# One chunk of offsets ahead of the first sampling, binarised weights beside the second, and the first convolution in half steps

## The chip, the core and the metric

The kernel runs on one NeuronCore of a Trainium2 chip. The metric is the device time of that core in microseconds (us), as the median of a kernel's executions that were not in a slow state. The kernel before takes 8729 us. A difference of less than 2% counts as "same". A stage length or a single wait below is read from one profiled execution of a kernel.

Engines: PE is TensorE (matmuls; PEld its weight loads), DVE is VectorE, ACT is ScalarE, POOL is GpSimd, SP is SyncE, which here only issues DMAs. "Granted clock" (PEclk) is the share of full speed that TensorE's throttle allowed. All data are fp32.

## The reference, cut to what matters

Four residual layers follow one another on `x` of shape (4, 256, 64, 64), each behind a group norm. Only the first and the weights of the third are touched by the change:

```python
# layer 0, per image (256 channels, 64x64 pixels)
y      = leaky_relu(bn(conv1x1(gn(x))))               # "first convolution"
xp     = y @ inproj_w.T + inproj_b                    # becomes the table that is sampled
t      = leaky_relu(bn(depthwise3x3(y)))
offset = t @ off_w.T + off_b;  mask = softmax(t @ mask_w.T + mask_b)   # 4 groups x 9 points
dout   = (grid_sample(pad(xp), ref + offset) * mask).sum(points)       # bilinear, by gathers
x2     = bn(y + dout @ outproj_w.T + outproj_b)
...                                                   # squeeze-excite, feedforward, residual
# layer 1: linear attention with a 5x5 depthwise convolution
# layer 2: a 3x3 convolution with binarised weights
scale  = mean(|w|, axis=(in, ky, kx)); b = scale * sign(w); c = clip(w, -1, 1)
bin_w  = (b - c) + c
# layer 3: non-local attention (softmax over pooled positions)
```

## The kernel before: the parts that matter

**The order of the whole.** A front (setup, binarising, first convolution and offsets of image 0) is followed by four sampling stages, one per image, and a tail without sampling. A sampling stage has 293 rounds; each round issues four gathers (indirect DMAs from POOL), 1172 in a stage. Other work goes beside it: `beside` takes, after each round, as many pieces from the generators of other work as their shares allow. Inside `ordered()` each engine executes in exactly this order.

```python
def beside(steps, number, *works):
    spent, open_ = [0] * len(works), set(range(len(works)))
    def advance(share):
        for j in sorted(open_):
            work, total, lo, hi = works[j]
            while j in open_ and lo <= share and spent[j] < total * (share - lo) / (hi - lo) or share >= hi:
                cost = next(work, None)          # one piece of work is emitted here
                if cost is None: open_.discard(j)
                if not cost: break               # 0: it has to wait for something
                spent[j] += cost
    for i, _ in enumerate(steps, 1):
        advance(i / number)
    ...

def prepare(images):
    pads, used = [], []
    n = len(images)
    return [((y for i in images for y in self.convolve(i, w, sp, bp, pads, used)), n * CONVOLVE, 0, 1 - 0.12 / n),
            (self.shifts(images, w["mw"], bp, pads, used), n * OFFSETS, 0.2 / n, 1)]

self.setup()
self.binarise()
beside(range(64), 64, *prepare([0]))                               # the front
with ordered():
    beside(self.sample(0, ssum[0]), rounds, *prepare([1, 2, 3]))   # sampling stage 0
    beside(self.sample(1, ssum[1]), rounds, *behind(0))            # stage 1, and so on
```

Note the condition of the `while`: it catches up. When the offsets had to wait (a piece of cost 0) and fall behind their share, all that is missing comes in one round.

**First convolution and offsets.** An image has eight blocks of 512 pixels and four chunks of 1024. Per block and half, the convolution makes two matmuls (four records in the trace) into a PSUM bank, a piece of the memory that matmuls write and ACT and DVE read. ACT and DVE take the result (leaky), the rows go into padded chunks, and a projection writes the table with sixteen DMAs.

```python
def convolved(b, x, yb, m):
    ps = self.ps()                                   # the pool of PSUM banks that all share
    for k in range(KT):
        nc.tensor.matmul(ps, cw[:, k, m*P:(m+1)*P], x[:, k], start=k == 0, stop=k == KT - 1)
    self.leaky(bp, yb[:, m], ps, sh[:, m:m+1], low[:, m:m+1])      # ACT, then DVE: at once
    self.spread({c: p[:, m] for c, p in own.items()}, rw(yb[:, m]), b, 1)
# projected(): two blocks of matmuls, DVE adds the bias, then per block
    for r in range(2):
        for s in range(2):
            for j in range(4):
                nc.sync.dma_start(tab[:, yi, 1:W+1, s, :]..., xo[...])   # 64 KB each

def offsets(...):                                    # per chunk
    for k in range(KT):
        yield from self.depthwise(...)               # DVE: 9 taps of 128x1024, three a piece
        nc.scalar.activation(t[:, k], acc, ...)      # ACT
        nc.vector.tensor_tensor(t[:, k], acc, t[:, k], ALU.max)
    for h in range(2):                               # PE: matmuls ps <- mw, t; DVE adds the bias
        ...
    yield from self.coordinates(...)                 # softmax, indices, weights; then one store
```

**The gathers.** `g` has seven buffers, so POOL may be seven rounds ahead of the matmuls that read them:

```python
g = self.gp.tile([P, G, 256], F32, name="g", bufs=7)
for i in range(G):
    nc.gpsimd.indirect_dma_start(out=g[:, i, :], in_=table, in_offset=...sl[:, r, i:i+1]...)
for x in range(2):
    for i in range(G):
        nc.tensor.matmul(acc[...], wm[...], g[:, i, x*P:(x+1)*P], start=x == 0, stop=x == 1)
```

**Binarising** is one load of 128x4608 elements, seven DVE operations of that size, 18 matmuls (36 records) over the columns and one store, ahead of everything else.

## Time and profile before

| | before |
|---|---|
| median of 4 executions | 8729.05 us (8709.94 to 8736.27) |
| profiled execution | span 8706.8 us, mean granted clock 0.836 |
| front (to the first gather) | 247.6 us |
| sampling stages 0, 1, 2, 3 | 1622.9, 1528.7, 1667.1, 1682.8 us |
| tail | 1957.7 us |

The profiled execution took 8708.86 us. It is none of the four, shorter than each of them and 20 us below their median; this matters when the traces are compared. A stage here runs from the end of the previous stage's last gather to the end of its own last gather. The page of the kernel before has the busy time of each engine and, below it, POOL's busy tenths in 40 equal slices; the third line is the costliest group, with busy us, mean ns and the idle time ahead of it:

```profile
PE 6339.9 (73%) x35276; PEld 3432.2 (39%) x35276; DVE 5243.8 (60%) x6279; ACT 2014.2 (23%) x4710; POOL 4578.5 (53%) x4694
...
POOL 0667767677777776777776557777755000000000
...
L520 POOL DMA_INDIRECT g<-tab,sl x4688 | 4577.8, 976 | 2169.9 <-issue 1295.2
```

No engine is full on average, so the averages do not give the bound. POOL's slices show the structure: an empty first slice (the front), then 30 slices at about 70% and an empty tail. The 70% are this kernel's full speed of gathering: 0.976 us of work and 0.3 us between two gathers, 1172 times, are about 1500 us.

The waits of PE, DVE and ACT in stage 0 (what each waited for; total us, number, longest):

```profile
ACT lk L166 <- PE ps L312: 365.7, 47, 16.0
DVE yc L167 <- ACT lk L166: 358.6, 44, 18.0
PE ps L414 <- DVE t L404: 263.5, 18, 15.8
```

The first two are the chain of the first convolution (matmul, ACT, DVE, each waiting for the one before); the third is PE waiting for a whole depthwise result. All three look expensive. Whether they cost anything is another question: only what stops POOL lengthens this stage.

### The profile page before, as it was taken

Reading aid. Unit: us, or ns where it says so; the run is one execution under the profiler, and the core shown is the slowest. Engines: PE = TensorE matmul, PEld = TensorE weight load, DVE = VectorE, ACT = ScalarE, POOL = GpSimd, SP = SyncE. Lnnn points to the kernel's source line nnn. Section 1 sums busy time; section 2 is a strip of 40 time slices with the busy share of each in tenths; the row PEclk is TensorE's granted clock in tenths of the full one; section 3 lists DMA queues with packets and bytes.
Section 4 is the critical chain, followed back from the end, with each engine's and each line's share of the span. In section 5 each row is a group of like instructions: output and inputs, shape, how many; then the busy total and the mean of one; then the engine's idle time right before and its main releaser. Section 6 shows DMA issues by size and latency. Waiting matters only on the chain. (4 is left out here: it accounts for less than half of the span.)

```text
span 8706.8 us, 92673 instructions
## 1 busy us (share of the span) xinstructions
PE 6339.9 (73%) x35276; PEld 3432.2 (39%) x35276; DVE 5243.8 (60%) x6279; ACT 2014.2 (23%) x4710; POOL 4578.5 (53%) x4694
## 2 busy tenths in 40 slices
PE   4645545569676677998767779897677898667887
PEld 2333322334333333444444434444444444334345
DVE  7445353342678775258777732778777268989213
ACT  1111111112222122222232322222322222222113
POOL 0667767677777776777776557777755000000000
PEclk7666766779767688999988989998888999889999
DMA  5556555554444454455544354555433211101210
GB/s 157 165 153 170 152 154 157 142 156 144 136 120 127 119 145 136 144 155 140 155 132 119 111 150 137 159 150 152 126 111 107 90 53 46 44 32 41 57 60 29
DMA packets 817660, 1052.57 MB, mean 121 GB/s; under 512 B 464064, under 2 KB 524608, under 8 KB 815424
## 3 DMA queue, kind: packets, MB, share of 16 engines
q0 software_dynamic: 225024, 614.77, 24.4%
q1 hardware_dynamic: 592192, 431.89, 17.3%
q8 instruction: 279, 4.57, 0.2%
q14 instruction: 165, 1.35, 0.0%
HBM read 878.36 MB, written 167.90 MB: 120 GB/s over the span
## 5 line engine op out<-in xcount | busy, mean ns | idle before, releaser
L520 POOL DMA_INDIRECT g<-tab,sl x4688 | 4577.8, 976 | 2169.9 <-issue 1295.2
L176 DVE SCALAR_TENSOR_TENSOR agg<-pad,vec,agg 128x1024 f32<-128x1024 f32 x2560 | 3295.3, 1287 | 69.1
L527 PE MATMUL acc<-g,wm 128*32 128x128 f32 x18752 | 1221.6, 319 | 1186.6 <-ACT at L532 762.0
L527 PEld LDWEIGHTS acc<-g,wm 128*32 128x32 f32 x18752 | 609.5, 121 | 1845.7 <-ACT at L532 984.7
L864 PE MATMUL ps<-xp,w 128*128 128x512 f32 x2304 | 1062.3, 608 | 80.7 <-DVE xp L848 52.8
L864 PEld LDWEIGHTS ps<-xp,w 128*128 128x128 f32 x2304 | 425.7, 192 | 565.5 <-issue 530.8
L552 ACT COPY dT<-dp 64x112 f32<-64x112 f32 x1176 | 287.1, 244 | 1328.9 <-PE dp L537 935.3
L511 DVE TENSOR_TENSOR wm<-con,sl 128x1024 f32<-128x1024 f32 (+1 forms) x296 | 357.5, 1208 | 223.5 <-PE acc L527 221.3
L645 PE MATMUL ps<-x2f,f 128*128 128x512 f32 x1024 | 477.3, 615 | 4.0 <-ACT f L636 4.0
L167 DVE SCALAR_TENSOR_TENSOR hm<-ps,vec,lk 128x512 f32<-128x512 f32 x256 | 192.2, 751 | 436.2 <-ACT lk L166 436.1
L652 PE MATMUL ps<-hm,f 128*128 128x512 f32 x1024 | 453.6, 597 | 0.0
L166 ACT ACTIVATE lk<-ps,low 128x512 f32<-128x512 f32 x320 | 219.8, 687 | 980.9 <-PE ps L645 558.2
L700 PE MATMUL ps<-xr,qw 128*128 128x512 f32 x768 | 418.1, 675 | 12.3 <-DMA xq<-x 3.2
L958 PE MATMUL pt<-ident,pe 128*128 128x128 f32 x1024 | 187.6, 330 | 228.2 <-ACT pe L950 226.1
L950 ACT ACTIVATE pe<-s,mx 128x512 f32<-128x512 f32 x256 | 173.8, 684 | 712.9 <-DVE mx L945 712.8
L414 PE MATMUL ps<-mw,t 128*128 128x108 f32 x512 | 96.5, 364 | 306.9 <-DVE t L404 306.9
L963 PE MATMUL ps<-gt,pT 128*128 128x128 f32 x2048 | 309.6, 314 | 5.6 <-ACT pT L959 3.1
L963 PEld LDWEIGHTS ps<-gt,pT 128*128 128x128 f32 x2048 | 287.9, 224 | 49.4 <-ACT pT L959 20.0
L653 DVE TENSOR_TENSOR xyf<-xyf,ps 128x512 f32<-128x512 f32 x64 | 44.0, 688 | 430.9 <-PE ps L652 430.9
L560 PE MATMUL po<-dT,ow 128*128 128x224 f32 (+1 forms) x1216 | 284.6, 383 | 24.6 <-DVE yb L564 13.2
L532 ACT COPY at<-acc 128x256 f32<-128x256 f32 (+1 forms) x588 | 218.5, 372 | 313.9 <-PE acc L527 304.8
L645 PEld LDWEIGHTS ps<-x2f,f 128*128 128x128 f32 x1024 | 192.1, 194 | 233.2 <-issue 224.5
(224 smaller groups left out, 7096.4 us busy)
## 6 DMA issues: line engine op xcount, KB each, us to landing
x<-x SPq DMA_DIRECT2D x160, 512.0 KB
g<-tab,sl POOLq DMA_INDIRECT x4688
xr<-x SPq DMA_DIRECT2D x96, 512.0 KB
x<-in_x SPq DMA_DIRECT2D x64, 512.0 KB
tab<-xo SPq DMA_DIRECT2D x512, 64.0 KB
y<-yc SPq DMA_DIRECT2D x32, 512.0 KB
x2f<-x SPq DMA_DIRECT2D x32, 512.0 KB
xyf<-x SPq DMA_DIRECT2D x32, 512.0 KB
```

Of the source, the lines that this page charges most:

```text
L166: nc.scalar.activation(t, ps, AF.Identity, bias=low, scale=SLOPE)
L176: nc.vector.scalar_tensor_tensor(acc, s, wt, acc, ALU.mult, ALU.add)
L511: nc.vector.tensor_tensor(wm[:, 0:nu], self.con("own").unsqueeze(1).unsqueeze(1).to_broadcast(sh), sl[:, r:r + nu, G:].unsqueeze(3).to_bro ...
L520: nc.gpsimd.indirect_dma_start(out=g[:, i, :], out_offset=None, in_=table, in_offset=bass.IndirectOffsetOnAxis(ap=sl.bitcast(I32)[:, r, i: ...
L527: nc.tensor.matmul(acc[32 * i:32 * i + 32, :], wm[:, r4, 4 * i + 2 * x:4 * i + 2 * x + 2, :], g[:, i, x * P:(x + 1) * P], start=x == 0, st ...
L552: nc.scalar.copy(dT[b][hs, :, q0:q0 + m * (v1 - v0)].rearrange("p g (v o) -> p g v o", o=m), dp[u][hs, v0:v1, :, s, 0:m].rearrange("p v g ...
L560: nc.tensor.matmul(po[m][:, 0:np_], self.ow[:, k, m * P:(m + 1) * P], dT[b][:, k, 0:np_], start=k == 0, stop=k == G - 1)
L645: nc.tensor.matmul(ps, f1[:, k, m * P:(m + 1) * P], x2[:, k], start=k == 0, stop=k == KT - 1)
L652: nc.tensor.matmul(ps, f2[:, k, m * P:(m + 1) * P], hm[:, k], start=k == 0, stop=k == 4 * KT - 1)
L700: nc.tensor.matmul(ps, qw[:, k, t * P:(t + 1) * P], x[:, k], start=k == 0, stop=k == KT - 1)
L864: nc.tensor.matmul(ps, w[:, k, t, m * P:(m + 1) * P], xp[:, k, t // 3:t // 3 + 8, t % 3:t % 3 + W], start=i == 0, stop=i == KT * 9 - 1)
L963: nc.tensor.matmul(ps[:, 0:P], pT[:, m], gt[:, m], start=m == 0, stop=m == 7)
```

## The change

It has four parts. (1) Only the first of image 0's four chunks of offsets is made in the front; the other three join the twelve of images 1 to 3 beside stage 0. (2) Binarising leaves the front, is cut into pieces of 128x768 and goes beside stage 1. (3) The first convolution is emitted in half steps: ACT and DVE take a matmul's result one step after it, and rows are spread two steps after. (4) Its matmuls get a PSUM bank of their own instead of one from the shared pool. The shares of the pacing and the hand-over of rows change along with these. The core of the diff:

```diff
-CONVOLVE, OFFSETS = NB * 17 + 18, NCH * 60
+CONVOLVE, OFFSETS, BINARY = NB * 9 + 26, 60, 62
@@ convolve
+        def after(lag, f, *args):
+            later.setdefault(now + lag, []).append(partial(f, *args))
         def convolved(b, x, yb, m):
-            ps = self.ps()
+            ps = self.ps1.tile([P, 512], F32, name="cv", tag="vk")
             for k in range(KT):
                 nc.tensor.matmul(ps, cw[:, k, ...], x[:, k], start=k == 0, stop=k == KT - 1)
-            self.leaky(bp, yb[:, m], ps, sh[:, m:m + 1], low[:, m:m + 1])
-            self.spread({c: p[:, m] for c, p in own.items()}, rw(yb[:, m]), b, 1)
+            t = bp.tile([P, 512], F32, name="lk")
+            after(1, lambda: nc.scalar.activation(t, ps, AF.Identity, ...))
+            after(1, lambda: nc.vector.scalar_tensor_tensor(yb[:, m], ps, ...))
+            after(2, spread, b, yb, m)
... (binarise in six parts with yields between; the loop over blocks as steps of cost 2)
@@ run
         self.setup()
-        self.binarise()
...
-            beside(range(64), 64, *prepare([0]))
+            pads, used = [], []
+            convolved = (y for i in range(1, N) for y in self.convolve(i, w, sp, bp, pads, used))
+            shifted = lambda first, last: (self.shifts(first, last, ...), (last - first) * OFFSETS)
+            beside(range(64), 64, (self.convolve(0, ...), CONVOLVE, 0, 1), (*shifted(0, 1), 0.3, 1))
             with ordered():
-                beside(self.sample(0, ssum[0]), rounds, *prepare(list(range(1, N))))
+                beside(self.sample(0, ssum[0]), rounds, (convolved, (N - 1) * CONVOLVE, 0, 0.96), (*shifted(1, N * NCH), 0, 1))
...
-            beside(self.sample(1, ssum[1]), rounds, *behind(0))
+            beside(self.sample(1, ssum[1]), rounds, (self.binarise(), BINARY, 0, 0.2), *behind(0))
```

## The prediction

> **What bounds the kernel now.** I read the per-stretch table of engine times first, cutting the span at the first gather (247.6 us) and at the four reductions of the channel sums (1885, 3438, 5117, 6800). Columns: length, then busy us and record count of PE, PE weight load, DVE, ACT, POOL; granted clock; DMA share; GB/s.
>
> ```profile
> 0.00:60.00 60.00, 9.89 (x36) 8.10 (x36) 32.83 (x27) 1.49 (x2) 0.70 (x6) 0.77 0.34 123
> 87.00:248.00 161.00, 87.75 (x291) 55.53 (x291) 145.21 (x198) 30.91 (x54) 0.43 (x1) 0.78 0.61 145
> 248.00:1885.00 1637.00, 889.60 (x6329) 523.67 (x6329) 726.34 (x977) 253.52 (x703) 1162.24 (x1183) 0.67 0.56 155
> 1885.00:3438.00 1553.00, 1126.83 (x6841) 554.96 (x6841) 998.18 (x970) 348.67 (x867) 1161.25 (x1190) 0.77 0.47 134
> ```
>
> See three things: a front of 248 us in which POOL, which issues the gathers, does nothing; DVE busy for 145 of the 161 us before the first gather; then four sampling stages, each near the time that POOL needs for its 1172 gathers. The tail after 6800 has no gather, and the change does not touch it. What a stage 0 (image 0's sampling) gather costs and loses is in the waits of POOL from 247 to 1885 us (total us, times, longest):
>
> ```profile
> POOL g L520 <- issue: 335.2, 1100, 0.3
> POOL g L520 <- DMA tab<-xo: 246.6, 2, 246.3
> POOL g L520 <- PE acc L527: 121.2, 22, 20.4
> ```
>
> 246.3 us is the front: the first gather waits for the last write of the table. The 335 us are the fixed 0.3 us between gathers. The 121 us are real stalls: all seven gather buffers full because PE stopped. In order of time over 960 to 1020 us one of them looks so:
>
> ```profile
> 985.53 0.76 PE L414 MATMUL ps<-mw,t 128*128 128x108 f32 x2 [15.73 <-DVE t L404]
> 999.83 5.89 PE L414 MATMUL ps<-mw,t 128*128 128x108 f32 x30 [13.53 <-DVE t L404]
> 1013.39 0.44 ACT L457 ACTIVATE ml<-ml 128x288 f32<-128x288 f32 x1 [14.88 <-DVE ml L456]
> 1016.62 1.02 POOL L520 DMA_INDIRECT g<-tab,sl  x1 [18.00 <-PE acc L527]
> ```
>
> A whole chunk of offsets stands at one place in the order: PE sits 15.7 + 13.5 us before its matmuls until DVE has the depthwise result, ACT then sits 14.9 us at the exponential, ahead of the copy that frees the accumulator. Seven rounds of gathers (about 35 us) hide most of it; 18 us come out. Following the source's pacing arithmetic round by round, whole or nearly whole chunks fall into one round at rounds 41, 60, 80, 134, 154, 173, 228, 248, 267, because the convolution hands over its rows late and the pacing then catches up. POOL's gaps over 0.6 us in stage 0 (9.1, 4.2, 9.1, 6.3, 18.0, 17.2, 5.9, 18.0, 20.4, 9.4 us) begin seven rounds after exactly these. Together 117.6 us; without them the stage is busy 1151.5 + small gaps 353.8 = 1505 us.
>
> **What the Trainium skill says.** (1) "PSUM — Partial Sum Buffer", Engine vs sequencer instructions: "ScalarE/VectorE/GpSimdE queues are strict FIFO", and matmuls start in program order. The stall above agrees. (2) "DMA: Bandwidth & Descriptors", Issuing engines are not separate DMA queues: the sequencer's time to initiate a DMA is usually small beside the DMA. Not here: the table is written by 128 DMAs of 64 KB per image, median issue 0.615 us, spaced about 0.655 us, so SP alone needs 16 x 0.655 = 10.5 us a block. (3) "VectorE: DVE Perf Modes", the perf-mode tier table: fp32 tensor_tensor and tensor_reduce at 1x, tensor_scalar at 2x. The trace agrees for the first and last (128x4608: 4.96 and 2.55 us); I use it for the new reduction. (4) The same PSUM page, The four PSUM rules: a matmul output takes at most one 2 KiB bank, 512 fp32 columns; so the convolution's own tile is a single bank that ACT and DVE must clear before the next convolution matmul. No trace of the kernel before tests this.
>
> **The change part by part.**
>
> *Binarising leaves the front.* The setup timeline is serial here:
>
> ```profile
> 12.82 4.96 DVE L244 SCALAR_TENSOR_TENSOR t<-w 128x4608 f32<-128x4608 f32 x1 [6.22 <-DMA w<-in_w2T]
> 53.12 0.35 SPq L257 DMA_DIRECT2D w<-s  x1
> 60.87 0.48 DVE L270 TENSOR_SCALAR dg<-ident,bn_r 128x128 f32<-128x128 f32 x2 [7.77 <-DMA w<-s]
> 63.53 18.33 SPq L147 DMA_DIRECT2D x<-in_x  x12
> ```
>
> The image loads start at 63.5 and the first convolution matmul at 87.4, 24 us later. In the new order the image loads follow the weight loads at about 5.6 us, so statistics end near 24. But the 48 zero writes of this image's table, which ran beside the binarising, now stand in SP's order between the statistics' loads and the reloads for the convolution: 4 x 5.16 = 20.6 us from about 17 us. So the convolution starts near 45, not at 30. Gain 42 us.
>
> *Only one chunk of offsets ahead.* A chunk costs DVE 18 taps x 1.29 = 23.2, two maxima x 1.22 = 2.4, bias adds 1.5, coordinates and weights about 12: 39 us. The convolution costs 16 x (0.746 + 0.747 + 0.684) = 34.8. Before, DVE had all of 161 us full. Now it needs 39 + 35 = 74 us, and SP becomes the limit: 10.5 us of table writes a block plus two stores and a load near 2 us, 12.5 us. From the fifth block on, each reload stands behind the table writes, and load latency (3), two passes through the single bank (each matmuls about 3, ACT 0.69, DVE 0.75), projection and adds come round in about 16 us. Sum: 45 + 14 to the first table write, 3 x 12.5, then 5 x 16 less a little, 2.5 to land: about 178, range 158 to 188. Against 247.6 the front gains about 68 us in all.
>
> *Stage 0.* Three chunks, 117 us of DVE work, enter a stage in which DVE is busy 726 of 1637 us: not a bound. What matters is the order. The new pacing (15 chunks spread from share 0; rows handed over earlier; half steps so that ACT and DVE take a matmul one step later) puts whole chunks in one round only at 236 (all of it), 251 (15 of 18 pieces) and ten pieces at 266; at 142 four pieces. By the measured likes: 18 to 20, 9.4, 0 to 3, 0, so near 28 us of stalls instead of 117.6. Gain 90 us.
>
> *Half steps.* ACT's and DVE's waits for the convolution in stage 0 (366 and 359 us) should nearly vanish. POOL set the pace in those rounds, so beyond the row hand-over this is worth nothing.
>
> *Binarising beside stage 1.* DVE: before 4.96 x 5 + 2.55 x 2 = 29.9 us; now plus a reduction of 4608 elements (1x, estimated 4.9 us from the 4.96 us row) and small-piece overhead: about 37 us, 12 loads of 384 KB and 6 stores, all in the first 59 rounds. DVE is 28% busy there, but PE is over 90% busy at a granted clock of 0.98 to 1.00 and POOL already loses some 14 us. In-order DVE waiting for a load holds up the leaky step behind it. Cost 12 us (0 to 30).
>
> Stages 2, 3 and the tail keep their program order: 0. Sum: 8729 - 68 - 90 + 12 = 8583; I say 8582.
>
> **The rivals.** (a) The front is not shortened to DVE's 74 us but to SP's chain; if reloads and the wait for the chunk's depthwise result add up, the first gather comes at 200 and the time is near 8605. For it: SP's order; against it: before, the first blocks' table writes started at 98.2, 112.5 and 130.5 us with DVE full. The other way, if the chain overlaps well, it comes at 155 and the total is near 8560. (b) Stalls turn up elsewhere: three more chunks make offsets denser (3.1 instead of 2.6 cost units a round), and PE's wait for t could remain in every chunk. Then half the stage 0 gain goes: 8625. Against: an ordinary piece is one per round, and seven rounds of buffers cover it. (c) Stage 1's dense feedforward becomes slower by 40 us, since PE is the second bound: 8610. (d) Everything overlaps, stage 0 stalls vanish and the front ends at 155: 8729 - 92 - 117 + 12, near 8530, over 2% faster. I give it one chance in five.
>
> **Range and chances.** The two gains are independent and each uncertain by 20 to 30 us; 8530 to 8635 should hold it 8 times in 10. The 2% line lies at 8729 x 0.98 = 8554, 28 us below my figure, so faster 0.23, same 0.74, slower 0.03.
>
> **What would show it.** First gather at 158 to 188 us with SP, not DVE, the last to be waited for; stage 0 from first to last gather near 1535 us (1623 now), with gaps after rounds 243 and 258 and none before round 100; PE's waits for t cut from 264 us to under 120; stage 1 at 1530 to 1560 (1528); stages 2, 3 and the tail within 5 us. I am wrong if the first gather comes after 200, if gaps of 5 us or more appear in early stage 0 or in the first 59 rounds of stage 1, or if later stages move.

## The result, and the profile after

The kernel after takes 8572.24 us (median of 4, 8560.74 to 8584.32) against 8729.05 us. The ratio is 0.9824, with a 95% interval of 0.9803 to 0.9845; it is the mean time of one kernel's fast runs over that of the other's of the same rounds, so not quite the ratio of the medians. That is 1.8% less, "same" by the 2% rule. The result is correct, and all runs were in the fast state. The prediction was 8582 us and "same": right, 10 us off.

By stages (us, one trace each; "stalls" is the sum of POOL's gaps over 0.6 us between two gathers of a stage):

| | before | after | difference | predicted |
|---|---|---|---|---|
| front | 247.6 | 184.7 | -62.9 | -68 |
| stage 0 (stalls) | 1622.9 (117.6) | 1522.4 (8.2) | -100.5 | -90 |
| stage 1 (stalls) | 1528.7 (29.9) | 1528.7 (23.4) | 0.0 | +12 |
| stage 2 | 1667.1 | 1666.0 | -1.1 | 0 |
| stage 3 | 1682.8 | 1693.2 | +10.4 | 0 |
| tail | 1957.7 | 1974.1 | +16.4 | 0 |
| span | 8706.8 | 8569.0 | -137.8 | -146 |

The medians differ by 157 us, the traces by 138: before's profiled execution (8708.86 us) was shorter than all of its timed ones, after's (8571.0 us) was an ordinary one.

The page of the kernel after, the same lines as shown of before:

```profile
PE 6457.6 (75%) x35252; PEld 3474.4 (41%) x35252; DVE 5259.4 (61%) x6319; ACT 2008.5 (23%) x4711; POOL 4583.8 (53%) x4694
...
POOL 1777777777777776777775567777654000000000
...
L561 POOL DMA_INDIRECT g<-tab,sl x4688 | 4583.1, 978 | 2010.6 <-issue 1484.2
```

The same gathers cost the same, 978 ns against 976. The idle time ahead of them fell from 2169.9 to 2010.6 us, by 159. That is the front and the stalls of stage 0 together (62.9 + 109.4), less small increases elsewhere.

The table of engine times by stretch, cut at the ends of the front's two halves and then of the stages (start:end, length, busy us and records of PE, PEld, DVE, ACT and POOL, granted clock, DMA share, GB/s):

```profile
46.00:184.70 138.70, 74.94 (x224) 43.16 (x224) 70.23 (x98) 26.32 (x48) 0.03 (x1) 0.82 0.67 155
184.70:1707.00 1522.30, 985.13 (x6342) 551.76 (x6342) 798.16 (x1059) 248.92 (x692) 1157.70 (x1172) 0.70 0.59 166
1707.00:3236.00 1529.00, 1102.26 (x6746) 546.91 (x6746) 1036.06 (x1016) 343.44 (x856) 1151.15 (x1173) 0.77 0.47 140
...
6595.00:8569.00 1974.00, 1576.59 (x5054) 851.66 (x5052) 1132.85 (x1524) 467.84 (x893) 0.00 (x0) 0.90 0.16 50
```

In the front DVE is now half busy (70 of 139 us), where the stretch that the prediction shows had it busy 145 of 161. Stage 0 has taken on 79 us of DVE work (798 us, 718.86 in the same stretch before) and is shorter all the same. Stage 1 has taken 40 us of DVE work (1036 against 996.55 us in the same stretch before) and has the same length. The last line is for later; the same stretch of the kernel before is this:

```profile
6749.10:8706.80 1957.70, 1559.91 (x5054) 842.38 (x5052) 1132.83 (x1524) 468.44 (x893) 0.00 (x0) 0.91 0.16 50
```

The waits of stage 0 after, of PE, POOL, DVE and ACT:

```profile
PE ps L455 <- DVE t L445: 46.2, 5, 13.5
...
POOL g L561 <- issue: 515.4, 1091, 183.4
POOL g L561 <- PE acc L568: 11.9, 13, 8.2
...
DVE yc L339 <- ACT lk L338: 107.7, 27, 11.4
ACT lk L338 <- PE cv L336: 56.7, 16, 10.8
```

PE's wait for a whole depthwise result went from 263.5 to 46.2 us, ACT's wait for the convolution from 365.7 to 56.7, and POOL's for PE from 121.2 to 11.9. (183.4 us of "issue" are the front: the profile found no event for what the first gather waited for. The end of the front, below, shows what it was.)

One burst of the old kind is left. In order of time, after:

```profile
1417.54 0.76 PE L455 MATMUL ps<-mw,t 128*128 128x108 f32 x2 [5.82 <-DVE t L445]
...
1431.83 5.20 PE L455 MATMUL ps<-mw,t 128*128 128x108 f32 x30 [13.54 <-DVE t L445]
...
1444.84 0.44 ACT L498 ACTIVATE ml<-ml 128x288 f32<-128x288 f32 x1 [14.32 <-DVE ml L497]
```

This is the chunk of round 236, which the prediction named; POOL lost 8.2 us at round 243, seven rounds later, and nothing anywhere else in the stage.

The front, in order of time (PE's first two records of the convolution), and the table writes of the front before and after (count; ns min/median/max; first to last start in us):

```profile
46.06 3.61 PE L336 MATMUL cv<-x,cwf 128*128 128x512 f32 x4 [15.68 <-DMA x<-in_x]
...
51.24 1.98 PE L336 MATMUL cv<-x,cwf 128*128 128x512 f32 x4 [1.56 <-DVE yc L339]
```
```profile
L333 SPq DMA_DIRECT2D tab<-xo x128: 574/615/2139, 98.2 to 244.4; - x128
```
```profile
L370 SPq DMA_DIRECT2D tab<-xo x128: 575/615/1485, 59.0 to 179.5; - x128
```

The first convolution starts at 46.06 us (87.4 before), the first table write at 59.0 (98.2 before), as predicted (45 and 59). The second record waits 1.56 us for DVE, which has to read the private bank before the next matmul may write it. The end of the front, from the timeline after:

```profile
168.14 12.01 SPq L370 DMA_DIRECT2D tab<-xo  x16
180.20 0.60 SPq L541 DMA_DIRECT2D sl<-sd  x1
...
183.74 2.36 DVE L552 TENSOR_TENSOR wm<-con,sl 128x1024 f32<-128x1024 f32 x2 [16.86 <-DMA sl<-sd]
184.67 1.27 POOL L561 DMA_INDIRECT g<-tab,sl  x1 [183.37 <-issue]
```

SP issues the last block's sixteen table writes for 12 us, and only then the load of the gathers' indices and weights (`sl`); DVE and the first gather start right after it lands. In e11, a second trace of this kernel, the profile names that load as what the first gather waited for.

### The profile page after: what moved, and what is told of

The parts are those of the page before. It is cut to its first block, busy times and chain, and to the rows that moved or that the text cites. A ratio compares the mean times of both kernels' runs of the same rounds, so it can differ in the third digit from the quotient of the medians.

```text
span 8569.0 us, 92678 instructions
## 1 busy us (share of the span) xinstructions
PE 6457.6 (75%) x35252; PEld 3474.4 (41%) x35252; DVE 5259.4 (61%) x6319; ACT 2008.5 (23%) x4711; POOL 4583.8 (53%) x4694
## 3 DMA queue, kind: packets, MB, share of 16 engines
q1 hardware_dynamic: 594496, 434.25, 17.4%
## 5 line engine op out<-in xcount | busy, mean ns | idle before, releaser
L561 POOL DMA_INDIRECT g<-tab,sl x4688 | 4583.1, 978 | 2010.6 <-issue 1484.2
L568 PE MATMUL acc<-g,wm 128*32 128x128 f32 x18752 | 1330.8, 320 | 1210.5 <-ACT at L573 628.7
L568 PEld LDWEIGHTS acc<-g,wm 128*32 128x32 f32 x18752 | 644.8, 121 | 1938.1 <-DMA g<-tab,sl 835.7
L601 PE MATMUL po<-dT,ow 128*128 128x224 f32 (+1 forms) x1216 | 293.6, 392 | 19.7 <-DVE yb L605 12.9
L166 ACT ACTIVATE lk<-ps,low 128x512 f32<-128x512 f32 x256 | 175.9, 687 | 557.0 <-PE ps L686 557.0
L693 PEld LDWEIGHTS ps<-hm,f 128*128 128x128 f32 x1024 | 190.6, 190 | 231.5 <-issue 231.1
```

The costliest lines, as they stand in the source:

```text
L561: nc.gpsimd.indirect_dma_start(out=g[:, i, :], out_offset=None, in_=table, in_offset=bass.IndirectOffsetOnAxis(ap=sl.bitcast(I32)[:, r, i: ...
L568: nc.tensor.matmul(acc[32 * i:32 * i + 32, :], wm[:, r4, 4 * i + 2 * x:4 * i + 2 * x + 2, :], g[:, i, x * P:(x + 1) * P], start=x == 0, st ...
L601: nc.tensor.matmul(po[m][:, 0:np_], self.ow[:, k, m * P:(m + 1) * P], dT[b][:, k, 0:np_], start=k == 0, stop=k == G - 1)
L693: nc.tensor.matmul(ps, f2[:, k, m * P:(m + 1) * P], hm[:, k], start=k == 0, stop=k == 4 * KT - 1)
```

## The experiments

There were twelve runs: e1 to e4 on one chip, e5 to e8 on a second, e9 to e12 on a third that turned out to be different (e11 and e12 are after and before again, unaltered). Each group has its own runs of the kernel before (medians 8722.26, 8716.34 and 9785.06 us), and ratios are to those. All results were correct. The timed runs were all in the fast state; e11 and e12 are single executions, whose state is unknown. Stage lengths in us:

| kernel | front | stage 0 (stalls) | stage 1 | stage 2 | stage 3 | tail | median, ratio to before |
|---|---|---|---|---|---|---|---|
| before | 247.6 | 1622.9 (117.6) | 1528.7 | 1667.1 | 1682.8 | 1957.7 | 8729.05 |
| after | 184.7 | 1522.4 (8.2) | 1528.7 | 1666.0 | 1693.2 | 1974.1 | 8572.24, 0.9824 |
| e1 | 230.2 | 1524.3 (8.7) | 1526.9 | 1672.8 | 1683.6 | 1954.8 | 8595.89, 0.9863 |
| e2 | 243.0 | 1545.3 (38.7) | 1533.8 | 1670.6 | 1688.6 | 1958.8 | 8638.38, 0.9907 |
| e3 | 189.3 | 1520.9 (9.7) | 1532.7 | 1672.8 | 1690.8 | 1962.9 | 8574.16, 0.9832 |
| e4 | 174.9 | 1517.9 (8.2) | 1531.9 | 1669.6 | 1696.3 | 1976.1 | 8568.54, 0.9830 |
| e5 | 238.5 | 1589.7 (82.8) | 1533.9 | 1673.0 | 1693.0 | 1960.3 | 8685.45, 0.9964 |
| e6 | 245.2 | 1518.5 (0.0) | 1523.7 | 1667.1 | 1688.6 | 1958.8 | 8605.49, 0.9879 |
| e7 | 176.7 | 1524.4 (8.2) | 1531.7 | 1669.6 | 1693.1 | 1972.3 | 8567.26, 0.9829 |
| e8 | 155.1 | 1519.6 (7.0) | 1538.8 | 1667.1 | 1682.8 | 1966.3 | 8543.74, 0.9811 |

The theory: the gain of stage 0 comes from emitting the offsets evenly, the front is bound by SP's issuing of DMAs, and half steps and the private bank are worth nothing of themselves. The rival: it is the half steps, which cut 300 us of ACT's and 250 us of DVE's waits in stage 0, that free POOL.

### e1: binarising back in the front

```diff
 def run(self):
     self.setup()
+    self.binarise()                    # its old body, whole
...
-    beside(self.sample(1, ssum[1]), rounds, (self.binarise(), BINARY, 0, 0.2), *behind(0))
+    beside(self.sample(1, ssum[1]), rounds, *behind(0))
```

> The changed kernel with the binarising of the second layer's weights put back in front, as before (and taken out of the second sampling stage). My theory: the 48 zero writes then run beside it again, the convolution starts at 87 us as in the kernel before instead of 46, the first gather comes near 226 us instead of 185, stage 1 (second sampling) stays at 1528 us. Time +41 us over the changed kernel, near 8613. Rival (binarising beside stage 1 costs there what it saves in front): within 10 us of the changed kernel, and stage 1 shorter than 1520.

Measured: 8595.89 us (8593.61 to 8602.98), ratio 0.9863 (0.9847 to 0.9879). The first matmuls of the convolution, by tile, in e1's front:

```profile
L317 PE MATMUL cv<-x,cwf x32: 592/592/1201, 88.7 to 119.0; 128*128 128x512 f32 x32
```

They start at 88.7 us instead of 46.1, and the first gather comes at 230.2 instead of 184.7: part 2 is worth 45.5 us in the front (42 predicted). Stage 1 without the binarising is as long as with it (1526.9 and 1528.7), so there the work is hidden and costs nothing measurable. Yet the median is 24 us above after's where 41 were expected, and only 22 to 27 us above those of e3 and e4, which ran in the same rounds with binarising moved: half of the 45 us does not reach the end. Stage 3 (1683.6 against 1690.8 and 1696.3) and the tail (1954.8 against 1962.9 and 1976.1) are shorter in e1; see the section on the later stages below.

### e2: all four chunks ahead again, everything else as after

```diff
-beside(range(64), 64, (self.convolve(0, ...), CONVOLVE, 0, 1), (*shifted(0, 1), 0.3, 1))
+beside(range(64), 64, (self.convolve(0, ...), CONVOLVE, 0, 1), (*shifted(0, NCH), 0.2, 1))
-    (convolved, (N - 1) * CONVOLVE, 0, 0.96), (*shifted(1, N * NCH), 0, 1))
+    (convolved, (N - 1) * CONVOLVE, 0, 0.96), (*shifted(NCH, N * NCH), 0.067, 1))
```

> The changed kernel with all four chunks of image 0's offsets ahead of the first sampling, and the pacing window of the rest as before; half steps, own bank and binarising beside stage 1 stay. By the pacing arithmetic whole or nearly whole chunks of offsets again fall into one round at rounds 48, 64, 79, 142, 157, 173, 236, 251, 266. My theory (bursts make the stalls): stage 0's gaps over 0.6 us come back after rounds 55, 71, 86, 149, 164, 180, 243, 258, 273, 60 to 110 us in all, stage 0 near 1600 us; the first gather moves from 185 to about 245 us (DVE full: 46 + 35 + 4 x 39). Time near 8572 + 60 + 80 = 8710. Rival (the half steps, not the even pacing, took the stalls away): stage 0 stays within 15 us of 1522, time near 8632.

Measured: 8638.38 us, ratio 0.9907 (0.9891 to 0.9924). The front is 243.0 us, only 4.6 less than before although binarising has left it: with four chunks ahead DVE's work takes the time that binarising leaves. DVE is busy 169 of the 197 us before the first gather. So parts 1 and 2 need each other in the front: alone they are worth 17.4 (e1) and 4.6 us, together 62.9. In stage 0 the offsets come in bursts again, POOL's stalls are 38.7 us in eight gaps, and PE waits 176.5 us for depthwise results. The expectation (60 to 110 us of stalls, 8710 us) was missed: the time is nearer to the rival's 8632, though the eight gaps begin at eight of the nine expected rounds, within a round. Of before's 117.6 us a third is back, not all, though the pacing is the old one for the offsets. Something else in the change takes the rest; e3 and e5 ask whether it is the half steps.

### e3: half steps undone

```diff
 def after(lag, f, *args):
-    later.setdefault(now + lag, []).append(partial(f, *args))
+    f(*args)
```

(The new padded chunk is then made ahead of the matmuls, with the same wait for a free one.)

> The changed kernel without half steps: matmul, ScalarE and VectorE parts of a convolution tile stand in one step again; one chunk ahead, own bank and binarising beside stage 1 stay. Bursts by the pacing arithmetic: 15 pieces at round 232, 11 at 247, 9 at 263. My theory: stage 0 gains nothing or little from half steps themselves: gaps 5 to 30 us in all against 8, stage 0 1520 to 1545, time within 25 us of 8572. Rival (half steps are what removed the 110 us): stage 0 over 1580, time over 8630. In ScalarE's and VectorE's waits for the convolution I expect a return to 300 us or more each, from 57 and 108.

Measured: 8574.16 us, ratio 0.9832 (0.9811 to 0.9853), the same as after. The waits of stage 0:

```profile
ACT lk L338 <- PE cv L336: 330.9, 48, 14.4
DVE yc L339 <- ACT lk L338: 199.2, 41, 13.0
```

ACT's wait for the convolution is back at 331 us (57 with half steps, 366 before), and POOL's stalls are 9.7 us instead of 8.2. So 270 us of ACT's waiting were removed and none of it was on the path: POOL has seven rounds of buffers, and ordinary pieces never use them up. The rival, in its simple form, falls.

### e4: the convolution in the shared pool of banks

```diff
-ps = self.ps1.tile([P, 512], F32, name="cv", tag="vk")
+ps = self.ps("cv")
```

> The changed kernel with the convolution's PSUM tile drawn from the shared ring of three instead of its own bank. My theory: within 8 us of 8572 in time, stage 0 within 5 us of 1522; the front could be some us shorter, because two convolution tiles can then be in flight (first gather 175 to 187). Rival (the own bank keeps the convolution from blocking the others' ring): stage 0's gaps grow to over 30 us.

Measured: 8568.54 us, ratio 0.9830 (0.9812 to 0.9849): no difference in time to after. The last matmul of the front's convolution starts at 129.9 us instead of 161.1, at a lower granted clock (0.75 against 0.82), so the private bank holds up the convolution: the next matmul waits until ACT and DVE have read the last one. The first gather comes at 174.9 us instead of 184.7. How much of these 10 us is the bank's is less sure, since the first gather of after itself moved by 8 us between two traces (e11); e10 below has 7 us on one chip. They are not seen at the end; stage 3 and the tail are the longest of all traces (1696.3 and 1976.1).

### e5: four chunks ahead and no half steps

The edits of e2 and e3 together.

> Four chunks ahead (bursts of whole offset chunks as in the run with four ahead) and no half steps. The two runs so far: bursts with half steps lost 38.7 us in stage 0, even pacing without half steps lost 9.7. My new theory: each of the two alone removes most of the 117.6 us of the kernel before, so with both undone stage 0's gaps return to 90 to 130 us, stage 0 near 1610, the first gather near 245, time near 8700. Rival (the kernel before lost them to something else, for example the shared PSUM ring or the row hand-over): gaps stay under 60 us and the time under 8660.

Measured: 8685.45 us (median of 8), ratio 0.9964 (0.9953 to 0.9974). Of stage 0's waits, POOL's for PE in e2, in e5:

```profile
POOL g L561 <- PE acc L568: 42.8, 21, 8.2
```
```profile
POOL g L563 <- PE acc L570: 87.4, 25, 17.1
```

With bursts, the half steps matter: without them POOL loses 82.8 us, with them 38.7. (The edit also shifts the bursts a little, but makes them no larger: by the arithmetic of the pacing loop, replayed from the source, the nine large ones hold 149 pieces in e2, 132 in e5 and 145 in before.) With even pacing they do not (9.7 and 8.2). So even pacing and half steps are two remedies for one thing, and after the first the second has nothing left to do. The 82.8 us are less than the 90 expected at the least and than before's 117.6; some 35 us of before's stalls come from what e5 does not undo (the row hand-over with its larger bursts, the shares or the private bank), and no run takes this apart further.

### e6: the kernel before, with bursts capped

Here nothing of the change is used. The old kernel's pacing loop takes at most two pieces of the offsets of images 1 to 3 in one round:

```diff
-                work, total, lo, hi = works[j]
+                work, total, lo, hi, *most = works[j]
+                taken = 0
                 while j in open_ and lo <= share and spent[j] < total * (share - lo) / (hi - lo) or share >= hi:
                     ...
                     spent[j] += cost
+                    taken += 1
+                    if most and share < hi and taken == most[0]:
+                        break
...
-    (self.shifts(images, w["mw"], bp, pads, used), n * OFFSETS, 0.2 / n, 1)]
+    (self.shifts(images, w["mw"], bp, pads, used), n * OFFSETS, 0.2 / n, 1) + ((2,) if n > 1 else ())]
```

> The kernel BEFORE with one edit: in the first sampling stage at most two pieces of the offsets are issued per round, so no whole chunk falls into one round; nothing else changes. My theory: stage 0's gaps go from 117.6 to under 20 us, stage 0 from 1623 to 1515 to 1535, first gather stays at 247.6, time 8729 - 100 = 8630. Rival (the front and the half steps carry the gain): stage 0 over 1590 and the time within 35 us of the kernel before.

Measured: 8605.49 us (8600.07 to 8615.04), ratio 0.9879 (0.9863 to 0.9896). POOL's waits in stage 0 and the front:

```profile
POOL g L520 <- issue: 335.1, 1099, 0.3
POOL g L520 <- DMA tab<-xo: 243.9, 1, 243.9
...
POOL g L520 <- PE acc L527: 2.1, 7, 0.3
```

There is no gap over 0.6 us in the whole stage. The front is untouched (245.2 us), and stage 0 is 1518.5 us long. A few lines of pacing give the whole gain of stage 0, and 111 us of the change's 157. The same pieces were issued, only never more than two at once, so this settles the cause of the stalls: it was the bursts.

### e7: the zero writes of the first table from POOL's queue

The prediction said that after the change the 48 zero writes delay the reloads for the convolution, and that SP's issuing bounds the table. e7 and e8 test one half each. Both are the kernel after with one edit.

```diff
+q = nc.sync if n else nc.gpsimd
-    nc.sync.dma_start(tab[g, 0, :, 0, :], z[0:TX, 0:64])
+    q.dma_start(tab[g, 0, :, 0, :], z[0:TX, 0:64])
... (all zero writes)
```

> The changed kernel with image 0's 48 zero writes issued by the idle GpSimd queue instead of SP, so that the reloads for the convolution don't stand behind them. My theory (SP's order sets the front): the first convolution matmul moves from 46 to about 32 us and the first gather from 185 to about 170; time -14 us, near 8558. Rival (data or VectorE sets the front): first gather stays over 181.

Measured: 8567.26 us, ratio 0.9829 (0.9812 to 0.9847): no difference in time. By tile, the convolution and the table writes:

```profile
L337 PE MATMUL cv<-x,cwf x64: 592/697/1222, 31.7 to 152.1; 128*128 128x512 f32 x64
```
```profile
L371 SPq DMA_DIRECT2D tab<-xo x128: 574/615/2314, 44.7 to 171.3; - x128
```

The convolution starts 14.4 us earlier (31.7 instead of 46.1), as the prediction had said it would without the zero writes (30). But the first gather comes only 8.0 us earlier: between the first table write and the first gather 132.0 us pass instead of 125.7. What took the 6 us is not shown. From the first convolution to the first gather PE was busy 80.6 us for 225 records here and 74.9 for 224 in after, at a granted clock of 0.75 and 0.82; e11, the same kernel as after, has 85.5 us at 0.74, and its front is 193.0 us. So a difference of 8 us between two fronts is no more than one kernel showed on two chips.

### e8: half of the table writes from POOL's queue

```diff
-                        nc.sync.dma_start(
+                        (nc.sync if n or s else nc.gpsimd).dma_start(
                             tab[:, yi, 1:W + 1, s, :].rearrange("g x c -> x g c"),
```

> The changed kernel with half of image 0's table writes (64 of 128 DMAs) issued by the idle GpSimd queue. My theory: SP's 0.655 us per table write sets the rate of the front, so the distance from the first table write to the first gather falls from 126 us to 80 to 100 us and the first gather comes at 140 to 160 us; time -30 us, near 8542. Rival 1 (the chain matmul, ScalarE, VectorE through one PSUM bank and the reload latency set the rate): under 10 us gained. Rival 2 (the software path is slower per write): the first gather comes later than 185.

Measured: 8543.74 us (8531.71 to 8556.75), ratio 0.9811 (0.9794 to 0.9829), unclear whether over 2%. The table writes of image 0, and the first gathers:

```profile
L370 SPq DMA_DIRECT2D tab<-xo x64: 574/628/2134, 59.7 to 150.0; - x64
L370 POOL DMA_DIRECT2D tab<-xo x64: 620/620/826, 60.0 to 140.1; - x64
L561 POOL DMA_INDIRECT g<-tab,sl x36: 942/946/1378, 155.1 to 199.5; - x36
```

The first gather comes at 155.1 us: 95 us after the first table write, against 126. Nothing else was changed, and the DMA engines moved more in that stretch (213 GB/s, 151 in after's), so it is SP's issuing, not the data's way, that bounds the front after the change. POOL takes 0.62 us for one such write, no longer than SP. Here much of the gain arrives: against e7, of the same call, the median is 24 us lower for 21.6 us in the front. Against after the medians differ by 28 us, but the ratios to each call's own before (0.9811 and 0.9824) only by some 11 us, and their intervals overlap.

### e9 and e10: all that helped, together

e9 is the kernel after with e7, e8 and e6's cap of two pieces. e10 is e9 with e4's shared bank.

> The changed kernel with image 0's zero writes and half of its table writes on the GpSimd queue, and at most two pieces of the offsets per round in the first sampling stage. From the single runs: the first gather at 155 with the table writes split, some 8 us earlier with the zero writes moved; the last 8 us gap of stage 0 gone. My theory: the parts add, first gather at 142 to 152, stage 0 near 1513, time 8525 to 8535. Rival (the parts share one limit): no faster than the run with split table writes, 8544.

> The same, and the convolution's PSUM tile from the shared ring, which alone brought the first gather 10 us forward. My theory: first gather at 130 to 145, time 8510 to 8525, over 2% faster than the kernel before. Rival (with the SP limit lifted the single bank no longer matters): within 4 us of the run without it.

These ran on a third chip, where the kernel before takes 9785.06 us, 12% more. Measured there: e9 9404.87 us, ratio 0.9604 (0.9586 to 0.9622); e10 9404.18 us, ratio 0.9610 (0.9594 to 0.9626). The first gather comes at 141.5 and 134.8 us: again the private bank costs 7 us of the front and nothing at the end (the rival of e10, at most 4 us in time, came true). Both first gathers are near the expected windows (142 to 152, 130 to 145), but the expected times (8510 to 8535) cannot be judged here. To compare with the change I needed it on this chip.

### e11 and e12: after and before once more, on the third chip

Both kernels unaltered, one execution each with a profile.

> The changed kernel again, unaltered, for a second trace. In the first one stage 3 took 1693 and the tail 1974 us against 1682 and 1958 of the kernel before, though their program is unchanged. My theory (spread from run to run): this trace gives other values, tail between 1955 and 1976, stage 3 between 1682 and 1696, without keeping both at the high end. Rival (the change slows the later stages): again 1690 or more and 1970 or more.

> The kernel before again, unaltered, for a second trace: the front 247 us and stage 0's gaps of 118 us should repeat within 2 us; the tail should lie between 1955 and 1976 and stage 3 between 1682 and 1696. If the later stages are a matter of spread, they differ from the first trace by some us here as well; if they repeat within 2 us, the changed kernel's slower tail is its own.

Measured: after 9488.45 us, before 9775.24 us. So after is at 0.970 of the 9785.06 of before (one run), and e9 and e10 are 0.9% below after: the combined version beats both kernels there, by about 84 and 380 us. On the first chips it did not run. The recorded expectations of e11 and e12 were missed: stage 0's gaps did not repeat (536.4 us for 118) and stage 3 lies far outside 1682 to 1696. They were meant to tell whether after's longer stage 3 and tail are its own; here these are 14.1 and 4.6 us longer than before's, in one execution each, which does not decide it.

| third chip | front | stage 0 (stalls) | stage 1 | stage 2 | stage 3 | tail |
|---|---|---|---|---|---|---|
| before (e12) | 247.4 | 2026.2 (536.4) | 1766.7 | 1874.5 | 1894.3 | 1964.4 |
| after (e11) | 193.0 | 1770.6 (280.5) | 1770.9 | 1874.7 | 1908.4 | 1969.0 |
| e9 | 141.5 | 1731.4 (237.3) | 1786.1 | 1888.6 | 1901.2 | 1968.0 |
| e10 | 134.8 | 1732.2 (236.2) | 1772.0 | 1887.9 | 1901.2 | 1968.0 |

The tail is as on the other chips, and so are before's front and, within 8 us, after's; the stages with gathers are longer, by some 210 to 250 us each after the change. POOL's waits in stage 0 of e12:

```profile
POOL g L520 <- PE acc L527: 349.4, 25, 42.2
POOL g L520 <- issue: 315.9, 1036, 0.6
POOL g L520 <- remote: 181.1, 76, 5.8
```

"remote", the profile's word for a releaser outside what it saw, stands nowhere in the traces of the first chips. A gather itself is as fast (982 ns mean on the page), and the gathers' DMA packets took the same 151 ns on average. But again and again no engine starts anything for a while: before had 156 intervals over 1.2 us in which no instruction started on the first chip and 622 here (234 and 989 us); over 2 us, well beyond the 1.28 us from gather to gather, 18 and 100 (56 and 310 us). What holds them up is open. The change is worth more here, 256 us in stage 0 instead of 100: the same bursts cost more when the gathers have no slack beside the pauses. That reading fits the longest wait (42.2 us here, 20.4 there) but was not tested by itself.

## Why the prediction was right, point by point

**Front: right, 63 us instead of 68.** Convolution and first table write came at 46.1 and 59.0 us (45 and 59 said). The first blocks followed at 13.2 and 12.9 us (12.5 said), the later ones at 16.6 to 19.5 (16 said), which sums to 184.7 instead of 178. The mis-sized term is "in about 16 us": the round through the single bank is longer, and without that bank (e4) the first gather came 10 us earlier. The granted clock, which the prediction left out, may enter too: e11, the same kernel at 0.74 instead of 0.82, ended its front 8 us later. SP as the bound was right: e8 takes half of SP's writes away and the front falls by 30 us.

**What moved from the front: less than said.** The prediction moved three whole chunks, "117 us of DVE work", into stage 0; it took on 79. The groups of depthwise operations in the front, before and after, tell why:

```profile
L176 DVE SCALAR_TENSOR_TENSOR agg<-pad,vec,agg 128x1024 f32<-128x1024 f32 x50 | 64.1, 1282 | 0.4
```
```profile
L176 DVE SCALAR_TENSOR_TENSOR agg<-pad,vec,agg 128x1024 f32<-128x1024 f32 x16 | 20.5, 1282 | 0.2
```

A chunk has sixteen of these. In the kernel before only three chunks and two operations had run when the first gather began; the fourth chunk already ran after it. So two chunks moved, not three. Since DVE does not bound stage 0 and SP bounds the front after, neither sum depended on it.

**Stage 0: right in cause, too small in size: 100 us instead of 90.** The chain "whole chunk in one round, PE and ACT stand, seven buffers run out" is shown by e6: the bursts alone removed, the stalls are 0.0. Of the three places named, round 236 cost 8.2 us ("18 to 20" said) and 251 nothing ("9.4"), so "near 28 us of stalls" was 8.2. The likes were measured in a kernel without half steps, and e2 against e5 shows that half steps halve what a burst costs; the step "half steps are worth nothing" was right only because hardly any bursts were left. Gathers' busy time and small gaps rose by 8.9 us together, which takes the 109 us of stalls to 100.

**Waits in stage 0: right.** ACT's and DVE's waits for the convolution fell to 57 and 108 us and gained nothing (e3). PE's wait for depthwise results fell to 46.2 us (under 120 said).

**Stage 1: wrong, 0 instead of 12 us.** The step that failed is "In-order DVE waiting for a load holds up the leaky step behind it": DVE waited for a load of the weights once, for 5.3 us, and POOL's stalls in the stage went from 29.9 to 23.4 us (e1, without the work, has 30.8). The DVE operations had the sizes said (six 128x768 reductions of 1034 ns, 6.2 us in all, for 4.9 estimated; 40 us more DVE work in the stage, for 37). DVE has room there: in the 307 us of the first 59 rounds or so it is busy 121 us (86 before).

**Stages 2, 3 and tail: "0" was wrong, +26 us in the first trace.** This is one of the prediction's own signs of being wrong ("if later stages move"). The program there is the same instruction for instruction. In the tail, as the two lines above show, PE has the same 5054 records, but is busy 1576.6 us instead of 1559.9, at a granted clock of 0.90 instead of 0.91, and the tail is longer by that. In stage 3 likewise: 8479 records, 1371 us of PE instead of 1352. Equal counts at more busy time and a lower clock show that TensorE's clock carries it. The clock records of the two traces know only full and half speed. In the tail it was half for 363.5 us in 49 stretches before, and for 399.4 us in 54 after; 36 us more at half speed cost about 18 us by estimate, near the 16.4 measured. In none of these stretches had PE been busy for more than 0.56 of the 4 us ahead of it (median 0.23 and 0.27; over the whole tail it is busy for 0.80), so they follow pauses of PE.

Why there were five more of them stays open. Over the ten traces of the first chips, the five kernels that reach the tail by 6607 us (after, e3, e4, e7, e8) have tails of 1962.9 to 1976.1, the five that reach it later 1954.8 to 1960.3; stage 3 is not parted so cleanly (1682.8 to 1696.3 and 1682.8 to 1693.0). So part of a gain in the first half may be handed back in the PE-bound second half. But this is one trace a kernel, where the times of one kernel already spread by 24 us (after), and stages 2 and 3 together took 3349.9 us both in before and in e8, the slowest and the fastest. Chance from run to run is not excluded. The other kernels give no rule either: e4's and e7's 8 to 10 us of front vanish in small increases of all later stages. The last term, 19 us in the other direction, is the choice of execution: before's trace was shorter than all its timed runs.

**The sum.** 68 + 90 - 12 = 146 was said. The traces give 62.9 + 100.5 + 0 - 25.7 = 137.8, the medians 157. Errors of 5 to 26 us with both signs cancelled, and the choice of execution took the rest: that the total is off by only 10 us is luck. The two large terms were right within 12%, and that is not.

**The rivals.** (a) and (b) did not happen: 184.7 is short of 200, and PE's waits did not remain. (c) did not happen. Half of (d) did, stage 0 almost without stalls; its other half, a front of 155 us, is what e8 reached by two queues.

## What to carry to other kernels

Where engines execute in order, ask of a stall first how much work was emitted in one place: here a pacing loop that catches up in one go cost 118 us, and a cap of two pieces per round removed all of it, whereas 270 us of waits that half steps removed were off the path. When work leaves a front, look for the next bound before counting the gain: here it was one queue's issuing of 128 small DMAs at 0.66 us each, and giving half to an idle engine's queue made the front another 30 us shorter. When a later, unchanged stage turns out longer, compare its busy time at equal counts and its granted clock before you blame its program (here 1576.6 against 1559.9 us for 5054 matmuls, at 0.90 and 0.91).

## What the Trainium skill lacked or had wrong

- "DMA: Bandwidth & Descriptors", Issuing engines are not separate DMA queues, calls the initiation time saved by several engines "usually small relative to the DMA itself". With 128 writes of 64 KB at 0.655 us spacing it was the bound: splitting them over two queues brought the first gather from 184.7 to 155.1 us (e8). That a sequencer can be the bound is said elsewhere, in "Perfetto Trace Analysis", What "DMA-bound" means; the sentence quoted leads away from it.
- No page was found that puts a number on what a single bank costs a chain (that independent matmul groups should rotate through banks is said in "Perfetto Trace Analysis", Matmuls): with one bank of its own the front's last convolution matmul started at 161.1 us, with the shared three at 129.9 (e4).
- No page was found that tells how in-order queues turn a burst of emitted work into stalls of other engines, nor how many buffers cover it: seven rounds of about 5 us did not cover a chunk at one place (117.6 us of stalls), and did when at most two pieces came in a round (0.0, e6).
- "TensorE: Matmul & The Clock Gate", What's actually happening, ties the clock to how busy PE has been recently. The traces agree in so far as half speed in the tail always came after little PE work (at most 0.56 of the 4 us before it, against 0.80 over the tail). The sentence does not tell whether 0.90 instead of 0.91 in the same tail is chance or follows from the faster part before it, and no run here does.
- No page was found on stretches in which none of a core's engines starts anything, of which one chip had many more: the same kernel took 8729 us on one chip and 9785 on another, at equal gather times (976 and 982 ns).
